# A four-layer graph network: strided sums in layer 0, own rows one tile ahead and an earlier check in layer 2

## The chip, the cores and the metric

The kernel runs on one core of one Trainium2 chip. The metric is device time in microseconds (us) of one execution. Five engines work side by side, each with its own queue of instructions kept in order: TensorE (PE, whose weight loads are shown apart as PEld), VectorE (DVE), ScalarE (ACT), GpSimd (POOL, which here issues the indirect DMAs) and SyncE (SP, which issues the plain ones). They wait for each other through semaphores.

## The reference

There are 3125 nodes with 128 features each and 100,000 edges, sorted by destination. Each edge has one of 500 relations, one of 8 types and three numbers. Four layers are applied in turn, each as `x = layernorm(x + layer(x))`:

```python
# layer 0: attention with 8 heads over a node's edges and the node itself
z_bar = segment_sum(z[edge_type], dst) / max(deg, 1)
pre_edge = (h @ P1)[dst] + (h @ P2)[src] + (z @ P3)[edge_type]
pre_self = h @ P1 + h @ P2 + z_bar @ P3
alpha = softmax of leaky(pre) @ y_w over the edges of dst and dst itself
t_edge = (h @ Wh)[src] + (z @ Wz)[edge_type];  t_self = h @ Wh + z_bar @ Wz
out = where(deg > 0, leaky(segment_sum(alpha * t) + residual_weight * h), h)
# layer 1: mean of x over the sources, then a two-layer perceptron
# layer 2: attention with 4 heads, one maximum for all edges
attn = leaky(sum(Q[dst] * K[src]) * SCALE + edge_attr @ We)
attn_exp = exp(attn - max(attn))
attn_norm = attn_exp / max(segment_sum(attn_exp, dst)[dst], 1e-12)
out = relu(concat([x, segment_sum(V[src] * attn_norm, dst) @ Wo + bo]) @ Wm + bm)
# layer 3: attention with one head; Q, K and V by node type, K also by edge type
```

Three sums over a node's edges in layer 0 matter here: that of the relations' rows z, for `z_bar`, made in two ways, and that of the weighted rows `alpha * t`.

## The kernel before, in words

The nodes are sorted by degree and padded to 3200, that is 25 tiles of 128 nodes, one node to a partition. A tile has as many slots for edges as its fullest node has edges: 57 for the first tile, 42, 40 and so on to 21 for the last, 821 in all. A chunk is eight slots (`W`); the last chunk of a tile may be smaller. Every layer goes through the 25 tiles in this order. `gather` (L89, whose instruction is L90) fetches one row per partition by an indirect DMA on POOL; `put` (L736, through `scatter`, L93) writes a tile's rows back by an indirect DMA. Edges beyond a tile's slots are worked through by `behind` (L641): a loop whose number of trips is loaded from memory (L647) and is zero for this input. The loop is still entered and left, and all engines meet at it.

A scheduler orders the instructions of every engine's queue from the program and its estimates of their times. Buffers come from pools; a tile of a pool with two buffers is written again only when its last but one user is done. In layer 0 the row buffers `hs` have eight, `zs` and most others two.

**Layer 0.** Beside its own work it counts edges between pairs of tiles for layer 1 (`counts`, L560 to L639, a generator that the main loop at L899 steps forward). Of each chunk the kernel gathers the rows of the sources into `hs`: 128 features for the logits, 128 for the message (the part `D:2 * D`) and 8 more. The relations' parts are made in two ways. In `gathered` (L801, 67 chunks, 45 of them full) rows `zs` are gathered from a table, added to `hs` (L808), and their last 64 columns are summed over the slots by `halved` (L809) and added to the tile's sum (L810). In `multiplied` (L819, 47 chunks, all full) one-hot matrices (L834, DVE) are multiplied by the relations (L838, PE) into `zT`, one block of 128 columns for each slot. PE then makes the logits' argument `pre` and the message's part `t_ps` (L849), which DVE adds to `hs` (L850). The eight blocks of `zT` are summed by L853, `halved` (L855) and, from a tile's second such chunk on, L857. Then come the logits (L787 to L790), the softmax (L669), and for each chunk `spread` (L868): the message part of `hs` is multiplied by the weights in place (L872), summed over the slots by `halved` (L873) and added to the tile's sum (L874). Then the tile's closing (L929 to L988) writes `x1` (the put at L977) and `u3`. The `prologue` of a tile (L768: a gather of x, its transpose at L711, two products) is called ahead of the last chunk of the tile before. `halved` is a tree of additions in place:

```python
while n > 2:
    k = n // 2
    V.tensor_add(v[:, :k], v[:, :k], v[:, n - k:n])
    n -= k
if n == 2:
    V.tensor_add(v[:, 0] if last is None else last, v[:, 0], v[:, 1])
```

For a full chunk that is four, two and one blocks: two instructions at L796 and one at L799. Elsewhere the kernel has a sum over the slots in one instruction, in `weigh` of layers 2 and 3 (`msg` at L696, the sum `u` at L700, its addition at L701).

**Layer 2.** It begins with a load of all edges' data (`pay_sb`, L1124) and 25 gathers of the tiles' own rows `xqb` (x and the query q; L1135). Then comes `behind` (L1166), then the loop over tiles (L1226): the query is prepared, rows `kv` are gathered by `rows2` (L1138), then logits, softmax and `weigh`. Last are `closing` (L1186), whose first transpose is that of `an` (L711, called at L1192), and `table3` (L1206), which makes the rows for layer 3 (L1222, L1223) and puts them (L1224). After the loop a check counts the nodes whose sum of weights, taken against the maximum over all nodes, falls under 1e-12 (L1249 to L1268). The count is loaded (L1269), and if it isn't zero, closings and tables are done again with the clamped sums (L1270); for this input it is zero. Layer 3 follows and reads the rows that were put.

Of the kernel before, what the change touches and what calls it, by code (L numbers as in the profile page):

```python
# [59 lines left out]
def segments(t):  # L60

    cs = chunks(t)
    n = -(-len(cs) // 5)
    runs = [cs[i * len(cs) // n:(i + 1) * len(cs) // n] for i in range(n)]
    return [(run[0][0], sum(run[-1]), run) for run in runs]
# [10 lines left out]
def tile_gnn(ctx, tc, a, out):  # L76
# [12 lines left out]
    def gather(dst, table, idx, **kw):  # L89
        return G.indirect_dma_start(out=dst, out_offset=None, in_=table, in_offset=indirect(idx), **kw)  # L90
# [612 lines left out]
    def query(ps, q):  # L703

        qp = ps.tile([P, D], F32, name="qp", bufs=2)
        A.activation(qp, q, AF.Copy)
        return qp
# [40 lines left out]
    with tc.tile_pool(name="l0", bufs=2) as wp, tc.tile_pool(name="l0s", bufs=1) as sp, \  # L748
# [40 lines left out]
            for s in range(k):  # L789
                T.matmul(lg_ps[:, s, :], low[:, s, :], yw8, start=True, stop=True)  # L790

        def halved(v, n, last=None):

            while n > 2:
                k = n // 2
                V.tensor_add(v[:, :k], v[:, :k], v[:, n - k:n])  # L796
                n -= k
            if n == 2:
                V.tensor_add(v[:, 0] if last is None else last, v[:, 0], v[:, 1])  # L799

        def gathered(h1T, idx, rl, n, za, lg_ps):  # L801

            hs = wp.tile([P, W, HC], F32, name="hs", bufs=8)
            zs = wp.tile([P, W, HC + R], F32, name="zs")
            for s in range(n):
                gather(hs[:, s, :], h_tab, idx(s))
                gather(zs[:, s, :], z_tab, rl[:, s:s + 1])
            V.tensor_add(hs[:, :n], hs[:, :n], zs[:, :n, :HC])  # L808
            halved(zs[:, :, HC:], n)  # L809
            V.tensor_add(za, za, zs[:, 0, HC:])  # L810
            for s0 in range(0, n, 4):
                k = min(4, n - s0)
                pre = ps.tile([P, 4, P], F32, name="pre")
                for s in range(k):
                    T.transpose(pre[:, s, :], hs[:, s0 + s, :D], ident)
                logits(pre, k, h1T, lg_ps[:, s0:s0 + k])
            return hs

        def multiplied(h1T, o, n, zbT, first, lg_ps):  # L819

            hs = wp.tile([P, W, HC], F32, name="hs", bufs=8)
            for s in range(n):
                gather(hs[:, s, :], h_tab, srcx[:, o + s:o + s + 1])
            rb = wp.tile([P, W * P], F16, name="rb")
            nc.sync.dma_start(rb[:, :n * P], rel_tab[o:o + n].rearrange("(o s) p -> o (s p)", o=1)
                              .to_broadcast([P, n * P]))
            zT = wp.tile([P, W * P], F32, name="zT")
            for s0 in range(0, n, 4):
                k = min(4, n - s0)
                cols = slice(s0 * P, (s0 + k) * P)  # L830
                oh = wp.tile([P, NK, 4 * P], BF16, name="oh")[:, :, :k * P]
                zps = ps1.tile([P, 4 * P], F32, name="zps")[:, :k * P]
                for i in range(NK):
                    V.tensor_scalar(oh[:, i], rb[:, cols], relid[:, i:i + 1], None, op0=OP.is_equal)  # L834
                    parts = [(zps, zq[:, i, :2 * R]), (zps[:R], zq[:, i, 2 * R:])]
                    for z, w in parts if i < NK - 1 else parts[::-1]:
                        whole = z is zps
                        T.matmul(z, w, oh[:, i], start=(whole and i == 0), stop=(whole and i == NK - 1))  # L838
                A.activation(zT[:, cols], zps, AF.Copy)
                pre = ps.tile([P, 4, P], F32, name="pre")  # L840
                T.matmul(pre[:, :k], zw[:, :D], zT[:, cols], start=True, stop=False)
                for s in range(k):
                    T.matmul(pre[:, s, :], hs[:, s0 + s, :D], ident, start=False, stop=(s == k - 1))  # L843
                logits(pre, k, h1T, lg_ps[:, s0:s0 + k])
            for s0 in range(0, n, 3):
                k = min(3, n - s0)
                t_ps = ps1.tile([P, 3, HC - D], F32, name="t_ps")
                for s in range(k):
                    T.matmul(t_ps[:, s, :], zT[:, (s0 + s) * P:(s0 + s + 1) * P], zw[:, D:], start=True, stop=True)  # L849
                V.tensor_add(hs[:, s0:s0 + k, D:], hs[:, s0:s0 + k, D:], t_ps[:, :k])  # L850
            assert n == W
            zh = wp.tile([P, W // 2, P], F32, name="zh")
            V.tensor_add(zh, zT.rearrange("z (s p) -> z s p", p=P)[:, :W // 2],  # L853
                         zT.rearrange("z (s p) -> z s p", p=P)[:, W // 2:])
            halved(zh, W // 2, zbT if first else None)  # L855
            if not first:
                V.tensor_add(zbT, zbT, zh[:, 0])  # L857
            return hs

        def masked(lg_ps, hss, n, mk):  # L860
# [7 lines left out]
        def spread(ac, hs, ex, n):  # L868

            val = hs[:, :n, D:2 * D]  # L870
            valh = val.rearrange("p s (h d) -> p s h d", h=H)
            V.tensor_tensor(valh, valh, ex.unsqueeze(3).to_broadcast([P, n, H, D // H]), op=OP.mult)  # L872
            halved(hs[:, :, D:2 * D], n)  # L873
            V.tensor_add(ac, ac, hs[:, 0, D:2 * D])  # L874

        def behind0(t, pl, mk, rl):
            _, _, h1T = prologue(t)
# [247 lines left out]
    with tc.tile_pool(name="l2", bufs=2) as wp, tc.tile_pool(name="l2s", bufs=1) as sp, \  # L1125
# [6 lines left out]
        l = sp.tile([P, NT, H2], F32, name="l")  # L1132
        V.memset(l, 0.0)
        V.memset(accb, 0.0)
        for t in range(NT):  # L1135
            gather(xqb[:, t, :], xq_tab, od.ids(t))

        def rows2(qp, pl, n, lg):  # L1138
            kv = wp.tile([P, W, 2 * D], F32, name="kv", bufs=8)
            for s in range(n):  # L1140
# [15 lines left out]

        def behind2(t, pl, mk, rl):
            lg = wp.tile([P, max(CAP), H2], F32, name="lg")
            kv = rows2(query(ps1, qb[:, t, :]), pl, W, lg[:, :W])
            biased(pl, W, lg[:, :W], mk)  # L1160
            ex = ps1.tile([P, max(CAP), H2], F32, name="ex")
            corr = softmax(wp, lg[:, :W], W, H2, m[:, t, :], l[:, t, :], ex[:, :W])
            faded(accb[:, t, :], corr, H2)
            weigh(wp, accb[:, t, :], kv[:, :, D:], ex[:, :W], W, H2)
# [41 lines left out]
        def table3(t):  # L1206
# [16 lines left out]
            A.activation(rows[:, :, D:], qkv[:, 2 * D:].unsqueeze(1).to_broadcast([P, NET, D]), AF.Copy)  # L1223
            put(ktv_tab, od, t, rows.rearrange("p e f -> p (e f)"))  # L1224

        for t in range(NT):  # L1226
            qp = query(ps1, qb[:, t, :])
            for s0, s1, run in segments(t):
                lg = wp.tile([P, max(CAP), H2], F32, name="lg")
                parts = []  # L1230
                for c0, w in run:
                    o = OFF[t] + c0
                    parts.append(rows2(qp, pay_sb[:, o:o + w], w, lg[:, c0 - s0:c0 - s0 + w]))
                n, o = s1 - s0, OFF[t] + s0
                biased(pay_sb[:, o:o + n], n, lg[:, :n], mask[:, o:o + n])
                ex = ps1.tile([P, max(CAP), H2], F32, name="ex")
                corr = softmax(wp, lg[:, :n], n, H2, m[:, t, :], l[:, t, :], ex[:, :n])
                faded(accb[:, t, :], corr, H2)
                for (c0, w), kv in zip(run, parts):
                    weigh(wp, accb[:, t, :], kv[:, :w, D:], ex[:, c0 - s0:c0 - s0 + w], w, H2)  # L1240

            rl = wp.tile([P, H2], F32, name="rl")
            V.tensor_scalar(rl, l[:, t, :], 1e-12, None, op0=OP.max)
            V.reciprocal(rl, rl)
            closing(t, rl)
            table3(t)


        mx = sp.tile([P, 1], F32, name="mx_all")  # L1249
        V.tensor_reduce(mx, m, AX.XY, OP.max)  # L1250
        mt = ps1.tile([P, P], F32, name="tp")
        T.transpose(mt, mx.to_broadcast([P, P]), ident)
        top = sp.tile([P, 1], F32, name="top")
        V.tensor_reduce(top, mt, AX.X, OP.max)
        f = sp.tile([P, NT, H2], F32, name="f")
        V.tensor_scalar(f, m, top, None, op0=OP.subtract)
        A.activation(f, f, AF.Exp)
        has2 = sp.tile([P, NT, H2], F32, name="has2")
        V.tensor_scalar(has2, l, 0.0, None, op0=OP.is_gt)
        V.tensor_mul(l, l, f)  # L1260
        few = sp.tile([P, NT, H2], F32, name="few")
        V.scalar_tensor_tensor(few, l, 1e-12, has2, op0=OP.is_lt, op1=OP.mult)
        few1 = sp.tile([P, 1], F32, name="few1")
        V.tensor_reduce(few1, few, AX.XY, OP.add)
        few_ps = ps1.tile([1, 1], F32, name="few_ps", tag="tp")
        T.matmul(few_ps, few1, ones[:, :1], start=True, stop=True)
        fewi = sp.tile([1, 1], I32, name="fewi")
        V.tensor_copy(fewi, few_ps)  # L1268
        again = nc.values_load(fewi, min_val=0, max_val=NP * H2)  # L1269
        with tc.If(again > 0):  # L1270
            V.tensor_scalar(l, l, 1e-12, None, op0=OP.max)
# [78 lines left out]
```

## Time and profile before

| what | us |
|---|---|
| median of 3 runs (lowest, highest) | 5862.23 (5854.55, 5864.28) |
| the profiled execution | 5814.11 |
| its span, first to last instruction | 5812.4 |
| sorting, tables, up to layer 0 | about 0 to 206 |
| layer 0 with its counts | about 206 to 3045 |
| layer 1 | about 3045 to 3223 |
| layer 2 | about 3223 to 4586 |
| layer 3 | about 4586 to 5812 |

The page gives an engine's busy time and share of the span. A group of instructions is a line of the kernel, an engine, an operation and the tiles it writes and reads; it shows its count, its total and mean duration, and what ended the idle time of the engine before it ("issue" is time in which nothing that the profile shows was waited for). Start times are us from the span's first instruction. The mean granted clock of TensorE is 0.588 of full speed. The times by stage are read from the timeline of the one profiled execution, which is 48 us below the median of the runs.

### The profile page before, as it was taken

The page shows a single profiled execution, that of the slowest core. Times are in us where ns is not written, and L with a number is a line of the kernel's source. Part 1 is how long each engine was busy: PE and PEld are TensorE (multiplying, and loading weights), DVE is VectorE, ACT ScalarE, POOL GpSimd, SP SyncE. Part 2 cuts the span into 40 slices and gives each one's busy share as a digit, 9 for nine tenths or more (in the row PEclk, how much of TensorE's full clock was granted, in tenths as well). Part 3 has the DMA queues.
Part 4 walks back from the last instruction along what each step waited for, and adds up shares of the span by engine and source line. Part 5 has one row for each costly group of instructions (what it writes and reads, how often), then busy time and mean ns, then how long its engine had stood idle before and what let it go on. Part 6 is the DMA issues. An engine that isn't in the chain of part 4 may idle for free. (4 is left out here: it accounts for less than half of the span.)

```text
span 5812.4 us, 36204 instructions
## 1 busy us (share of the span) xinstructions
PE 2236.2 (38%) x10027; PEld 1363.8 (23%) x10027; DVE 3104.1 (53%) x6976; ACT 934.1 (16%) x2437; POOL 3074.3 (53%) x3136
## 2 busy tenths in 40 slices
PE   7165545555556556576658112222233200000000
PEld 5143333333334334344433001111111100000000
DVE  8354555554455446565652346565656455545555
ACT  1031222221222222222211001111111100000000
POOL 0555545545453544444640566566656366666664
PEclk9565556555665666566569555555555555555555
DMA  2423322322222222222335333333333233333332
GB/s 80 120 75 85 88 75 76 86 74 80 74 81 70 80 76 79 82 76 79 102 92 196 106 95 107 99 110 114 104 100 107 72 96 92 90 93 93 94 89 66
DMA packets 220239, 530.60 MB, mean 91 GB/s; under 512 B 65690, under 2 KB 112461, under 8 KB 215386
## 3 DMA queue, kind: packets, MB, share of 16 engines
q0 software_dynamic: 147968, 437.97, 26.6%
q1 hardware_dynamic: 72024, 89.90, 4.7%
q8 instruction: 87, 1.43, 0.1%
q14 instruction: 160, 1.30, 0.1%
HBM read 457.09 MB, written 70.63 MB: 91 GB/s over the span
## 5 line engine op out<-in xcount | busy, mean ns | idle before, releaser
L90 POOL DMA_INDIRECT hs<-h_tab,srcx x821 | 880.0, 1072 | 602.1 <-issue 448.7
L90 POOL DMA_INDIRECT kv<-kv_tab,pay_sb x821 | 782.1, 953 | 421.7 <-issue 239.5
L90 POOL DMA_INDIRECT kv<-ktv_tab,pay_sb x821 | 778.8, 949 | 332.3 <-issue 258.1
L90 POOL DMA_INDIRECT zs<-z_tab,rel x445 | 466.8, 1049 | 695.4 <-DVE az L810 303.3
L628 PE MATMUL c_ps<-c_ohs,c_ohd 128*128 128x128 bf16 x1300 | 334.3, 410 | 299.1 <-issue 110.3
L700 DVE TENSOR_REDUCE u<-msg 128x128 f32<-128x1024 f32 (+4 forms) x228 | 384.2, 1685 | 114.3 <-remote 69.6
L838 PE MATMUL zps<-oh,zq 128*128 128x512 bf16 x752 | 339.7, 516 | 88.3 <-DVE oh L834 80.1
L790 PE MATMUL lg<-yw,low 128*128 128x8 f32 x1642 | 306.4, 316 | 125.8 <-ACT low L788 81.6
L790 PEld LDWEIGHTS lg<-yw,low 128*128 128x128 f32 x1642 | 305.2, 276 | 162.8 <-ACT low L788 104.0
L628 PEld LDWEIGHTS <-c_ohd 128*128 128x128 bf16 x1300 | 187.2, 147 | 431.7 <-issue 256.2
L1295 DVE TENSOR_TENSOR qk<-kv,qp 128x1024 f32<-128x1024 f32 (+4 forms) x114 | 126.4, 1109 | 289.1 <-DMA kv<-ktv_tab,pay_sb 242.8
L623 DVE TENSOR_TENSOR c_ohs<-c_ends,c_up 128x1024 bf16<-128x1024 bf16 (+4 forms) x193 | 118.9, 616 | 248.0 <-remote 111.8
L696 DVE TENSOR_TENSOR msg<-kv,ex 128x1024 f32<-128x1024 f32 (+4 forms) x228 | 249.1, 1104 | 0.0
L604 ACT ACTIVATE c_oha<-c_oha,srclo 128x50 bf16<-128x50 bf16 (+2 forms) x821 | 201.5, 327 | 258.8 <-DVE c_oha L600 189.5
L850 DVE TENSOR_TENSOR hs<-hs,t_ps 128x408 f32<-128x408 f32 x141 | 74.5, 528 | 300.2 <-remote 193.0
L787 DVE TENSOR_TENSOR low<-pre,h1T 128x512 f32<-128x512 f32 (+1 forms) x215 | 141.3, 660 | 166.9 <-PE pre L843 76.1
L630 ACT ACTIVATE c_sb<-c_ps 128x512 bf16<-128x512 f32 (+1 forms) x175 | 96.5, 552 | 802.2 <-remote 363.0
L1143 DVE TENSOR_TENSOR qk<-kv,qp 128x1024 f32<-128x1024 f32 (+4 forms) x114 | 126.1, 1107 | 181.6 <-DMA kv<-kv_tab,pay_sb 173.1
L849 PE MATMUL t_ps<-zw,zT 128*128 128x136 f32 x752 | 153.7, 338 | 151.1 <-issue 105.1
L711 PE MATMUL tp<-ident,xk 128*128 128x128 f32 x100 | 42.3, 423 | 426.7 <-DVE xk L1211 88.6
L711 PE MATMUL tp<-ident,an 128*128 128x128 f32 x25 | 11.5, 461 | 434.5 <-DVE msg L696 174.3
L788 ACT ACTIVATE low<-low 128x512 f32<-128x512 f32 (+1 forms) x215 | 128.9, 606 | 274.7 <-DVE low L787 246.1
(394 smaller groups left out, 5252.7 us busy)
## 6 DMA issues: line engine op xcount, KB each, us to landing
c_tab<-c_sb SPq DMA_DIRECT2D x25, 768.0 KB
cs<-c_tab SPq DMA_DIRECT2D x6, 3200.0 KB
hs<-h_tab,srcx POOLq DMA_INDIRECT x821
kv<-kv_tab,pay_sb POOLq DMA_INDIRECT x821
kv<-ktv_tab,pay_sb POOLq DMA_INDIRECT x821
rb<-rel_tab SPq DMA_DIRECT2D x47, 256.0 KB
zs<-z_tab,rel POOLq DMA_INDIRECT x445
h_tab<-h SPq DMA_DIRECT2D x25, 132.0 KB
```

The lines of the kernel that those rows point to most:

```text
L90: return G.indirect_dma_start(out=dst, out_offset=None, in_=table, in_offset=indirect(idx), **kw)
L604: A.activation(oha[:, s, 0, :], oha[:, s, 1, :], AF.Copy, scale=srclo[:, o:o + 1])
L628: T.matmul(cps[:, j * P:(j + 1) * P], ohd[:, :, nb * j + i], ohs[:, :, nb * j + i], start=(i == 0), stop=(i == nb - 1))
L696: V.tensor_tensor(msg[:, :n, :].rearrange("p s (h d) -> p s h d", h=heads), val.rearrange("p s (h d) -> p s h d", h=heads), ex.unsqueeze(3 ...
L700: V.tensor_reduce(u, msg[:, :n, :].rearrange("p s d -> p d s"), AX.X, OP.add)
L787: V.tensor_add(low[:, :k], pre[:, :k], h1T.unsqueeze(1).to_broadcast([P, k, P]))
L788: A.activation(low[:, :k], low[:, :k], AF.Relu)
L790: T.matmul(lg_ps[:, s, :], low[:, s, :], yw8, start=True, stop=True)
L838: T.matmul(z, w, oh[:, i], start=(whole and i == 0), stop=(whole and i == NK - 1))
L849: T.matmul(t_ps[:, s, :], zT[:, (s0 + s) * P:(s0 + s + 1) * P], zw[:, D:], start=True, stop=True)
L1143: V.tensor_mul(qk[:, :n], kv[:, :n, :D], qp.unsqueeze(1).to_broadcast([P, n, D]))
L1295: V.tensor_mul(qk[:, :n], kv[:, :n, :D], qp.unsqueeze(1).to_broadcast([P, n, D]))
```

## The change

It has three parts. In layer 0, `halved` is replaced by `summed`, a single reduction over the slots with the slots as innermost axis, read with a stride, into a small tile of its own (`zr`, `zh`, `hr`; the first `zT` chunk of a tile goes straight to `zbT`). The addition to the tile's sum stays; for `zT` the first halving, which was written apart as L853, is within the reduction now. In layer 2, the 25 gathers of own rows no longer stand in front of `behind`: tile 0's stands ahead of the loop over tiles, and that of tile t + 1 follows the query of tile t; the body of `behind` gathers its own. And the check becomes a function that is called in the last tile of the loop, in front of that tile's `closing`.

```diff
@@ layer 0
-        def halved(v, n, last=None):
-
-            while n > 2:
-                k = n // 2
-                V.tensor_add(v[:, :k], v[:, :k], v[:, n - k:n])
-                n -= k
-            if n == 2:
-                V.tensor_add(v[:, 0] if last is None else last, v[:, 0], v[:, 1])
+        def summed(to, rows):
+
+            V.tensor_reduce(to, rows.rearrange("p s d -> p d s"), AX.X, OP.add)
...
-            halved(zs[:, :, HC:], n)
-            V.tensor_add(za, za, zs[:, 0, HC:])
+            zr = wp.tile([P, R], F32, name="zr")
+            summed(zr, zs[:, :n, HC:])
+            V.tensor_add(za, za, zr)
...
-            zh = wp.tile([P, W // 2, P], F32, name="zh")
-            V.tensor_add(zh, zT.rearrange("z (s p) -> z s p", p=P)[:, :W // 2],
-                         zT.rearrange("z (s p) -> z s p", p=P)[:, W // 2:])
-            halved(zh, W // 2, zbT if first else None)
+            zh = zbT if first else wp.tile([P, P], F32, name="zh")
+            summed(zh, zT.rearrange("z (s p) -> z s p", p=P))
             if not first:
-                V.tensor_add(zbT, zbT, zh[:, 0])
+                V.tensor_add(zbT, zbT, zh)
...
-            halved(hs[:, :, D:2 * D], n)
-            V.tensor_add(ac, ac, hs[:, 0, D:2 * D])
+            hr = wp.tile([P, D], F32, name="hr")
+            summed(hr, val)
+            V.tensor_add(ac, ac, hr)
@@ layer 2
-        for t in range(NT):
-            gather(xqb[:, t, :], xq_tab, od.ids(t))
...
         def behind2(t, pl, mk, rl):
             lg = wp.tile([P, max(CAP), H2], F32, name="lg")
+            gather(xqb[:, t, :], xq_tab, od.ids(t))
...
+        def check():
+
+            mx = sp.tile([P, 1], F32, name="mx_all")
...
+            V.tensor_copy(fewi, few_ps)
+            return f, fewi
+
+        gather(xqb[:, 0, :], xq_tab, od.ids(0))
         for t in range(NT):
             qp = query(ps1, qb[:, t, :])
+            if t + 1 < NT:
+                gather(xqb[:, t + 1, :], xq_tab, od.ids(t + 1))
             for s0, s1, run in segments(t):
...
+            if t == NT - 1:
+                f, fewi = check()
             closing(t, rl)
             table3(t)
...
-        mx = sp.tile([P, 1], F32, name="mx_all")
...
-        V.tensor_copy(fewi, few_ps)
         again = nc.values_load(fewi, min_val=0, max_val=NP * H2)
```

The lines left out in `check()` are those of the check before, unchanged.

More of the change, by code (lines that the diff above doesn't have):

```diff
@@ L1224, in table3 @@
             put(ktv_tab, od, t, rows.rearrange("p e f -> p (e f)"))
+        def check():
+            mx = sp.tile([P, 1], F32, name="mx_all")
+            V.tensor_reduce(mx, m, AX.XY, OP.max)
+            mt = ps1.tile([P, P], F32, name="tp")
+            T.transpose(mt, mx.to_broadcast([P, P]), ident)
+            top = sp.tile([P, 1], F32, name="top")
+            V.tensor_reduce(top, mt, AX.X, OP.max)
+            f = sp.tile([P, NT, H2], F32, name="f")
+            V.tensor_scalar(f, m, top, None, op0=OP.subtract)
+            A.activation(f, f, AF.Exp)
+            has2 = sp.tile([P, NT, H2], F32, name="has2")
+            V.tensor_scalar(has2, l, 0.0, None, op0=OP.is_gt)
+            V.tensor_mul(l, l, f)
+            few = sp.tile([P, NT, H2], F32, name="few")
+            V.scalar_tensor_tensor(few, l, 1e-12, has2, op0=OP.is_lt, op1=OP.mult)
+            few1 = sp.tile([P, 1], F32, name="few1")
+            V.tensor_reduce(few1, few, AX.XY, OP.add)
+            few_ps = ps1.tile([1, 1], F32, name="few_ps", tag="tp")
+            T.matmul(few_ps, few1, ones[:, :1], start=True, stop=True)
+            fewi = sp.tile([1, 1], I32, name="fewi")
+            V.tensor_copy(fewi, few_ps)
+            return f, fewi
+        gather(xqb[:, 0, :], xq_tab, od.ids(0))
         for t in range(NT):
             qp = query(ps1, qb[:, t, :])
+            if t + 1 < NT:
+                gather(xqb[:, t + 1, :], xq_tab, od.ids(t + 1))
             for s0, s1, run in segments(t):
@@ L1244, in tile_gnn @@
             V.reciprocal(rl, rl)
+            if t == NT - 1:
+                f, fewi = check()
             closing(t, rl)
             table3(t)
-        mx = sp.tile([P, 1], F32, name="mx_all")
[L1250 to L1267, printed above, removed]
-        V.tensor_copy(fewi, few_ps)
         again = nc.values_load(fewi, min_val=0, max_val=NP * H2)
```

## The prediction

> **What bounds the kernel now.** I read the page first, then stages, waits, order of time. The page's totals fit no engine as the bound:
>
> ```profile
> PE 2236.2 (38%) x10027; PEld 1363.8 (23%) x10027; DVE 3104.1 (53%) x6976; ACT 934.1 (16%) x2437; POOL 3074.3 (53%) x3136
> ```
>
> The sums belong to layer 0 (206 to about 3045 us). The chain of waits is followed back only to 3220 us, so layer 0 is read from windows: busy us of PE, PEld, DVE, ACT, POOL in each 500 us.
>
> ```profile
> 500.00:1000.00 500.00, 287.99 (x1408) 189.08 (x1408) 279.39 (x657) 126.01 (x335) 243.58 (x229) 0.60 0.29 80
> 2500.00:3000.00 500.00, 322.73 (x1468) 210.25 (x1466) 292.14 (x806) 123.90 (x313) 268.84 (x258) 0.62 0.34 91
> ```
>
> No engine reaches two thirds: the period of a tile is set by queues kept in order that wait for each other in turn. The waits of layer 0 (total, times, longest):
>
> ```profile
> POOL hs L90 <- issue: 448.7, 778, 46.5
> POOL zs L90 <- DVE az L810: 303.3, 17, 30.8
> ...
> PE tp L711 <- DMA x<-in_x,node_d: 102.2, 7, 25.4
> ...
> PE zps L838 <- DVE oh L834: 80.1, 16, 13.2
> ```
>
> POOL stands until DVE has freed a row buffer; PE then stands for the x rows that POOL gathers behind those rows, and for a one-hot (L834) that stands on DVE behind a tile's sums. DVE's timeline shows such a burst (start, duration):
>
> ```profile
> 1523.21 2.35 DVE L872 TENSOR_TENSOR hs<-hs,lgs 128x1024 f32<-128x1024 f32 x2
> 1525.48 1.95 DVE L796 TENSOR_TENSOR hs<-hs 128x512 f32<-128x512 f32 x4
> 1527.35 0.48 DVE L799 TENSOR_TENSOR hs<-hs 128x128 f32<-128x128 f32 x2
> 1527.76 0.28 DVE L874 TENSOR_TENSOR az<-az,hs 128x128 f32<-128x128 f32 x1
> ...
> 1534.18 0.35 DVE L834 TENSOR_SCALAR oh<-rb,relid 128x512 bf16<-128x512 f16 x1
> ```
>
> By start times, four L796 take 1.87 us and two L799 0.41: 1.14 us per chunk of eight slots. The first L874 ends at 1528.04; POOL's next row gather starts at 1528.78. The L834 ends at 1534.53, PE's zps starts at 1534.58 after 12.3 us of waiting. So DVE's burst is on the path in some tiles, and POOL's rows and x in the others.
>
> **What the Trainium skill says.** "VectorE: DVE Perf Modes", section "The perf-mode tier table (the rule you actually need)", gives tensor_reduce its 1x mode alone, as it does fp32 tensor_tensor. The trace agrees: over 1024 contiguous elements, a reduce takes 1211 ns (L1296), a multiply 1217 (L872). "SBUF — State Buffer", section "Specifications (TRN2)", has 16-byte lines with a penalty for each crossing to a new one. A reduce over slots crosses at every element, and here it is dearer:
>
> ```profile
> L700 DVE TENSOR_REDUCE u<-msg 128x128 f32<-128x1024 f32 x184 | 344.0, 1869 | 101.6 <-remote 64.7 <-issue 23.3 <-DVE msg L696 7.3
> L1296 DVE TENSOR_REDUCE lg<-qk 128x8 f32<-128x1024 f32 x92 | 111.4, 1211 | 32.5 <-remote 13.6 <-issue 10.2 <-DVE lg L681 3.4
> L796 DVE TENSOR_TENSOR hs<-hs 128x512 f32<-128x512 f32 x92 | 61.5, 682 | 0.0
> ```
>
> "Perfetto Trace Analysis", section "Optimizing Scalar/DVE Operations", has some 60 ns of overhead per DVE instruction, with about half the profiled latency overlapped by the next. That speaks for fewer instructions, and the trace agrees: L874 lasts 281 ns, the next starts after 0.20 us.
>
> **Part 1, layer 0's sums.** Removed: the halvings (L796, L799) and the zh add (L853). Added: one strided reduce each. The nearest row is L700, the same operation, axis and size: 1869 ns for 1024 elements, 1012 for 512. Successors start about 0.08 us before a predecessor's end, so they occupy 1.78 and 0.93 us of the queue.
> - hs, 92 full chunks: 1.78 - 1.14 = 0.64 each, 59 us. 22 partial ones, priced as four slots: 0.93 - (0.33 + 0.20) = 0.40 each, 9 us.
> - zT, 47 chunks: 1.78 - (0.61 + 0.33 + 0.20) = 0.64 each, 30 us.
> - zs, 45 full chunks of 512 elements: 0.93 - (0.33 + 0.20 + 0.13) = 0.27 each, 12 us; 22 partial ones at half that, 3 us.
>
> Together 113 us more of DVE, although some 408 instructions go (two fewer in most chunks). Bounds: at L1296's rate the sums would cost 1.13 us against 1.14 and the part nothing; the row means without overlap (+0.48 us x 92 and so on) give 79. I take 113, since L700's form is the same.
>
> How much is on the path? Following layer 0's timeline backwards tile by tile I put about a half of it on PE and 28% on DVE, with some 60 to 77% of the halvings in those DVE stretches; but a delay there is partly taken up by a wait with another releaser. I choose a half: +56 us. Against it, the new order of DVE interleaves two multiplies and the sum: the first buffer comes free after 2 x 1.13 + 1.78 = 4.04 us of a burst instead of 2 x 1.13 + 1.87 + 0.41 + 0.20 = 4.74, 0.7 us earlier. Over 24 tiles that is 17 us where POOL's wait decides, and I take half: -8. The changed program also has other orders: POOL puts a tile's remaining rows ahead of the next x gather, by 2 to 8 gathers in about half of the first twelve tiles (1.25 us each), but its last zs gathers before the x1 put; PE's transpose of x stands later in tiles 7 to 15. Each can help or hurt: 0, with +/-35 us for the range. Layer 0: **+48**.
>
> **Part 2, layer 2's own rows.** Before, all 25 gathers stand on POOL ahead of the loop's entry, which waits until the last has landed; then come the first edge rows:
>
> ```profile
> 3249.68 8.48 DMA xqb<-xq_tab,node_d
> ...
> 3262.02 0.66 issue
> 3262.68 0.94 POOL kv L90
> ```
>
> Gathers start 1.25 us apart, 3223.33 to 3253.44. In the changed order POOL meets the loop first, then 12 own-row gathers, 57 rows, 1, 32, 12, and so on. DVE's `left` (L646), which the loop's trip loading follows, ends at 3226.0. In layer 3 the same ends at 4589.15 and rows start at 4592.45: 3.3 us. So gathers could start at 3229.3 and edge rows 12 x 1.25 later, at 3244.3: 18 us earlier. If the entry also waits for the 2463 KB load of pay_sb (issued 3222.52, landed by 3230 to 3233), it is 11 to 14. I take **-14**. The other 13 gathers, 16.3 us of POOL, stand by row 90 and later; POOL waits 19.12 us at tile 0's put (3455.58) for rows whose chain left POOL at row 81 (3362.82), so they are hidden. Were that cover gone, they would cost up to 16 and the part be about nil.
>
> **Part 3, the check.** Before, it runs beside the last rows (L1222, 4576.5), the put and its landing, 4577.92 to 4583.01; its result (4579.31) is awaited by nobody, since POOL goes on only after the landing: moving it saves 0. After, its PE transpose and matmul stand ahead of the last closing's transpose of `an`, and its DVE block ahead of that closing's L1202; ACT loads tables for its exp.
>
> ```profile
> 4559.84 0.12 PE tp L711
> ...
> 4577.92 5.09 DMA ktv_tab<-rows,node_d
> ```
>
> Its DVE chain lasts about 2.2 us (4577.09 to 4579.31) and can start once the previous tile's rows (L1222) end at 4560.56; then `an`'s transpose stands at about 4562.7 instead of 4559.8: **+3**, between 0 (it runs in DVE's idle time) and +5 (two table loads of 1.28 us shown). Behind it are ACT's copies, PE's projections and the put.
>
> **Sum:** 48 - 14 + 3 = +37. The profiled execution is 5814.11 us (span 5812.4), so 5851 on its scale; it is 48 us below the median of the runs, 5862.23, to which I add the difference: **5899**.
>
> **Rivals.**
> 1. Hidden sums, which ends on the other side. If the loop of POOL's rows, x and PE sets each tile, DVE's extra work fills its 45% idle time and the earlier release counts in full: -17 - 14 + 3 = -28, 5834. For: 448.7 us of POOL's waits and PE's 102.2 for x. Against: PE's waits for L834, at the end of bursts that grow by 0.64 us x 4 chunks. It decides where under (17 + 14 - 3)/113, a quarter, of the added time is on the path.
> 2. Full cost: the chain through DVE closes in every tile, +113 - 14 + 3 = +102, 5964. For: POOL's 303.3 us for DVE's L810, which the dearer zs sum precedes. Against: the x waits.
> 3. They cancel: a sixth on the path (+19) and -8, -14, +3 give 0, 5862. The change then does what it says and nothing is seen of it.
>
> **Numbers.** A measurement of this kernel can tell about 0.2% (12 us) from no change. Forecast 0.45 (own range 5872 to 5935), hidden 0.27, full 0.14, cancelled 0.14. Faster: 0.23 of the hidden case and 0.02 of the cancelled, 0.25. Same: 0.01, 0.04 and 0.07, 0.12. The rest, 0.63, slower. The range from 5836 to 5955 leaves out about 0.12 of the hidden case and 0.08 of the full one.
>
> **What would show it.** Right: strided sums of 1.85 us in layer 0 for hs and zT, DVE's busy time there up by about 80 us, layer 0's end about 48 us later; the first edge row of layer 2 about 14 us sooner after the first own row's former start, and POOL's 19 us wait at the first put kept or grown; the last put 3 us later after the previous tile's rows. Wrong: sums near 1.2 us; a tile period unchanged while DVE's busy share grows; own rows that wait for something else and delay the edge rows; or a layer 0 that moves by more than 35 us through POOL's and PE's new order alone.

## The result, and the profile after

The changed kernel takes 5906.24 us (median of 6 runs, 5892.24 to 5933.12), the kernel before 5855.52 us beside it (6 runs): ratio 1.0092, 95% interval 1.0073 to 1.0111, slower by some 54 us on the ratio (the medians alone are 51 us apart). The profiled execution of the changed kernel takes 5892.24 us, its span is 5890.4. That is 78 us more than the profiled execution before, whose time lay below all six runs of its kernel above; shares of the difference are taken from ratios, traces serve to find the places.

The page's first lines after (busy us, share, instructions):

```profile
PE 2226.4 (38%) x9959; PEld 1369.5 (23%) x10027; DVE 3229.0 (55%) x6568; ACT 936.2 (16%) x2438; POOL 3009.5 (51%) x3136
```

DVE has 408 instructions less and is busy 125 us longer. The groups of the new sums, by shape (count, total us, mean ns):

```profile
L794 DVE TENSOR_REDUCE hr<-hs 128x128 f32<-128x1024 f32 x92 | 181.6, 1986 | 0.0
...
L794 DVE TENSOR_REDUCE zr<-zs 128x64 f32<-128x512 f32 x45 | 48.1, 1070 | 0.0
L794 DVE TENSOR_REDUCE zbT<-zT 128x128 f32<-128x1024 f32 x25 | 47.4, 1895 | 51.6 <-issue 47.0 <-ACT zT L835 4.6
L794 DVE TENSOR_REDUCE zh<-zT 128x128 f32<-128x1024 f32 x22 | 42.4, 1927 | 0.0
```

These are as dear as L700, that of hs somewhat dearer. A burst at the end of a tile on DVE's timeline:

```profile
1534.28 2.35 DVE L866 TENSOR_TENSOR hs<-hs,lgs 128x1024 f32<-128x1024 f32 x2
1536.55 3.85 DVE L794 TENSOR_REDUCE hr<-hs 128x128 f32<-128x1024 f32 x2
1540.32 0.28 DVE L869 TENSOR_TENSOR az<-az,hr 128x128 f32<-128x128 f32 x1
...
1547.64 0.58 DVE L794 TENSOR_REDUCE hr<-hs 128x128 f32<-128x384 f32 x1
...
1548.54 0.34 DVE L830 TENSOR_SCALAR oh<-rb,relid 128x512 bf16<-128x512 f16 x1
```

The first one-hot (L830, before L834) comes 14.3 us after the burst's start, before it came 11.0 us after. The first buffer is free when the first L794 ends, about 1538.5, 4.3 us after the burst's start (before 4.8); POOL's next row gather starts at 1539.26. Two stretches of layer 0, columns as before:

```profile
500.00:1000.00 500.00, 272.44 (x1366) 183.17 (x1374) 289.27 (x556) 118.40 (x311) 229.79 (x225) 0.60 0.28 78
...
2500.00:3000.00 500.00, 286.69 (x1325) 187.44 (x1337) 277.69 (x644) 116.63 (x302) 220.04 (x227) 0.62 0.30 82
```

The last stretch shows the loss: PE does 287 us of work in it instead of 323. The waits of layer 0 (206 to 3110 us):

```profile
POOL hs L90 <- issue: 537.0, 792, 40.2
...
POOL zs L90 <- DVE zr L794: 396.5, 34, 37.2
...
PE zps L834 <- DVE oh L830: 81.9, 15, 18.2
...
PE tp L711 <- DMA x<-in_x,node_d: 19.8, 1, 19.8
```

Such a list splits a wait by the instruction that ended it, and a changed program gives it other names. The groups on the two pages have the whole idle time in front of POOL's gathers (after the second bar), first before, then after:

```profile
L90 POOL DMA_INDIRECT hs<-h_tab,srcx x821 | 880.0, 1072 | 602.1 <-issue 448.7
L90 POOL DMA_INDIRECT zs<-z_tab,rel x445 | 466.8, 1049 | 695.4 <-DVE az L810 303.3
```

```profile
L90 POOL DMA_INDIRECT hs<-h_tab,srcx x821 | 833.6, 1015 | 673.5 <-issue 537.0
L90 POOL DMA_INDIRECT zs<-z_tab,rel x445 | 445.6, 1001 | 650.9 <-DVE zr L794 396.5
```

In front of the row gathers `hs` POOL stands 71 us longer. In front of `zs` it stands 45 us less in all, though the part put down to DVE's sum of `zs` has grown (303 to 397). PE's wait for the x rows has nearly gone as a name (102 to 20 us); all idle time in front of that transpose fell by less, from 160 to 119 us. PE's wait for the one-hot has not grown (80 and 82 us). Stages, from the starts of the puts in the two traces (us):

| | before | after | difference |
|---|---|---|---|
| last x1 put of tile 16 (layer 0) | 2468.7 | 2467.6 | -1 |
| last x1 put of layer 0 | 3040.9 | 3108.3 | +67 |
| first edge row of layer 2 | 3262.7 | 3317.1 | +54 |
| first put of layer 2 | 3455.6 | 3511.0 | +55 |
| second put of layer 2 | 3525.7 | 3602.8 | +77 |
| third put of layer 2 | 3566.8 | 3636.1 | +69 |
| last put of layer 2 | 4577.9 | 4652.7 | +75 |
| last put of layer 3 | 5803.1 | 5881.2 | +78 |

Layer 0 lost all its time behind tile 16, although most of DVE's added work lies before it. In these last tiles DVE's waits whose releaser the trace can't name (remote) grew from 45 to 130 us. Layer 2 won 13 us at its first edge row, was 10 us behind at its second put, and 2 us behind at its third.

### The profile page after: what moved, and what is told of

It is laid out like the page before. It is cut to its first block, busy times and chain, and to the rows that moved or that the text cites. A ratio compares the mean times of both kernels' runs of the same rounds, so it can differ in the third digit from the quotient of the medians.

```text
span 5890.4 us, 35699 instructions
## 1 busy us (share of the span) xinstructions
PE 2226.4 (38%) x9959; PEld 1369.5 (23%) x10027; DVE 3229.0 (55%) x6568; ACT 936.2 (16%) x2438; POOL 3009.5 (51%) x3136
## 5 line engine op out<-in xcount | busy, mean ns | idle before, releaser
L90 POOL DMA_INDIRECT hs<-h_tab,srcx x821 | 833.6, 1015 | 673.5 <-issue 537.0
L90 POOL DMA_INDIRECT zs<-z_tab,rel x445 | 445.6, 1001 | 650.9 <-DVE zr L794 396.5
L700 DVE TENSOR_REDUCE u<-msg 128x128 f32<-128x1024 f32 (+4 forms) x228 | 384.2, 1685 | 131.4 <-remote 76.4
L834 PE MATMUL zps<-oh,zq 128*128 128x512 bf16 (+1 forms) x696 | 316.8, 520 | 87.7 <-DVE oh L830 81.9
L794 DVE TENSOR_REDUCE hr<-hs 128x128 f32<-128x1024 f32 (+4 forms) x114 | 202.4, 1786 | 0.0
```

Of the source, the lines that this page charges most:

```text
L700: V.tensor_reduce(u, msg[:, :n, :].rearrange("p s d -> p d s"), AX.X, OP.add)
L794: V.tensor_reduce(to, rows.rearrange("p s d -> p d s"), AX.X, OP.add)
```

## The experiments

They ran on chips that differ. On most of them the kernel before takes 5815 to 5872 us (the first kind), on one 5145 to 5166 us (the second kind). Every ratio is taken against the kernel before, run beside it on the same chip.

### The parts one by one

Layer 0's sums alone: the diff's first four hunks on the kernel before.

> Layer 0's strided sums alone, layer 2 as before. If the sums carry the whole difference and layer 2's two parts cancel, 5855 + 54 = 5909 (ratio 1.009). If layer 2 gains what the forecast said (-14 + 3), the sums alone must cost more: 5920 (1.011). Under 1.006 would mean that layer 2 itself makes the changed kernel slower.

Measured: 5859.95 us against 5815.48, ratio 1.0076 (1.0056 to 1.0097). The sums make nearly all of it, as the first case has it; 1.011 is excluded.

The own rows alone:

```diff
-        for t in range(NT):
-            gather(xqb[:, t, :], xq_tab, od.ids(t))
...
+        gather(xqb[:, 0, :], xq_tab, od.ids(0))
         for t in range(NT):
             qp = query(ps1, qb[:, t, :])
+            if t + 1 < NT:
+                gather(xqb[:, t + 1, :], xq_tab, od.ids(t + 1))
...
```

> Layer 2's own-row gathers alone. Forecast's reason (13 later gathers hidden behind POOL's wait at the first put): -14, ratio 0.9976, first edge row 13 to 14 us sooner and every put of layer 2 as much sooner. Rival, gain given back: the first edge row is sooner, but from tile 1 on the puts stand where they stood, ratio 1.000; in the changed kernel's trace the puts' lead of 12 us at tile 0 was gone at tile 1. Second rival: that loss belonged to that one execution, in which DVE and ACT had gaps of about 1 us between instructions for 45 us, and is not seen here.

Measured: ratio 0.9999 (0.9988 to 1.0011), 5814.50 us; a gain of 14 us (0.9976) is excluded. The gaps named as the second rival came again at the same instructions with the same lengths, so they do not belong to one execution. Against the last x1 put, the first edge row starts 208.3 us later instead of 221.8, and the first put 402.4 instead of 414.7; the second put stands 494.8 us later instead of 484.8, the third 528.0 instead of 525.9.

The check alone, with its lines moved into `check()` unchanged:

```diff
...
+            if t == NT - 1:
+                f, fewi = check()
             closing(t, rl)
             table3(t)
```

> The check's move alone. Forecast's reason: +3 us on the path from the last closing to the last put, ratio 1.0005, only to be seen in the trace: the last closing's transpose of an stands behind the check's matmul. Rival: it runs in idle time of DVE and PE, 0.

Measured: ratio 1.0012 (1.0002 to 1.0022), 5821.17 us: slower, by 1 to 13 us. The interval holds the 3 us of the forecast. PE's timeline around the last closing shows them, before:

```profile
4556.29 3.55 PE L1221 MATMUL e_ps<-wed,kT 128*128 128x512 f32 x4 [0.78 <-ACT kT L713]
4559.67 0.27 PE L711 MATMUL tp<-ident,an 128*128 128x128 f32 x1
```

and in the changed kernel:

```profile
4628.72 1.98 PE L1214 MATMUL e_ps<-wed,kT 128*128 128x512 f32 x4 [0.92 <-ACT kT L713]
4630.54 0.27 PE L1224 MATMUL tp<-ident,mx_all 128*128 128x128 f32 x1
4633.19 0.19 PE L1238 MATMUL few_ps<-ones,few 128*1 128x1 f32 x2 [2.38 <-DVE few L1236]
4633.62 0.33 PE L711 MATMUL tp<-ident,an 128*128 128x128 f32 x1 [0.24 <-DVE fewi L1240]
```

Before, the transpose of `an` follows the e_ps matmuls directly. If it did so here, it would stand where that of `mx_all` stands, at 4630.54; it waits for DVE's check and starts at 4633.62.

### Duration or order

The sums' duration can be changed with the order kept, if each full sum reads eight neighbouring columns (near reads): the traces show the same sequence of instructions as in the changed kernel on DVE (6568), ACT (2438) and POOL (3136). On PE some records are missing from one of the traces; in the repeat below the sequence is the same there too.

```diff
-            V.tensor_reduce(to, rows.rearrange("p s d -> p d s"), AX.X, OP.add)
+            n = rows.shape[1]
+            if n == 8:
+                V.tensor_reduce(to.rearrange("p (s g) -> p s g", s=8), rows.rearrange("p s (g e) -> p s g e", e=8), AX.X, OP.add)
+            else:
+                V.tensor_reduce(to, rows.rearrange("p s d -> p d s"), AX.X, OP.add)
```

> The changed kernel, whose sums over eight slots read eight neighbouring columns instead of one column of eight slots (a different sum: layer 0's relation sums and messages are then not the reference's; the addresses read and their number are the same). The order of instructions is that of the changed kernel on every engine; only the durations of these sums fall, from 1.99, 1.9 and 1.07 us to some 1.2, 1.2 and 0.65. Theory 1, duration: half of 113 us was on the path, so it returns to about 5855 - 11 = 5845, ratio 0.997 to 1.000. Theory 2, order: the new order of PE, ACT and POOL in layer 0 makes the loss (the trace of the changed kernel lost its time in tiles 17 to 23 alone), so it stays at 5900, ratio 1.008 to 1.010. Between: a share for each.

Measured: ratio 1.0042 (1.0028 to 1.0056), 5838.97 us. The full sums of hs fell to 1208 ns (group by shape), and DVE's busy time stands in the page's first line:

```profile
L796 DVE TENSOR_REDUCE hr<-hs 128x128 f32<-128x1024 f32 x92 | 110.0, 1208 | 0.0
```

```profile
PE 2240.8 (38%) x10027; PEld 1364.4 (23%) x10027; DVE 3110.9 (53%) x6568; ACT 934.4 (16%) x2438; POOL 3013.0 (52%) x3136
```

All sums together take 221.5 us instead of 343.8. About half of the loss went with the 122 us; the other half stayed, although DVE is busy no longer than with the halvings (3110.9 and 3104.1 us). Neither theory alone.

The opposite: the order of the kernel before, with dearer halvings (the same sequence on DVE, ACT and POOL as before).

```diff
-                V.tensor_add(v[:, :k], v[:, :k], v[:, n - k:n])
+                lo, hi = v[:, :k], v[:, n - k:n]
+                if k >= 2:
+                    lo, hi = (q.rearrange("p s d -> p d s") for q in (lo, hi))
+                V.tensor_add(lo, lo, hi)
...
-            V.tensor_add(zh, zT.rearrange("z (s p) -> z s p", p=P)[:, :W // 2],
-                         zT.rearrange("z (s p) -> z s p", p=P)[:, W // 2:])
+            V.tensor_add(zh.rearrange("z s p -> z p s"), zT.rearrange("z (s p) -> z p s", p=P)[:, :, :W // 2],
+                         zT.rearrange("z (s p) -> z p s", p=P)[:, :, W // 2:])
```

> The kernel before and its order of instructions, with the halvings of four and two blocks (and zh's first) going through their elements slots innermost, so that each takes longer by its strides; results as before. From the reduction, strides cost (1986 - 1208)/1024 = 0.76 ns for each element read; a chunk's 768 additions would cost 0.6 to 1.2 us more, all chunks together 90 to 190 us of DVE. If a quarter of DVE's added time is on the path, as in the changed kernel with and without near reads (0.5% or 29 of 122 us), ratio 1.004 to 1.008. If a half is, as forecast, 1.008 to 1.016. If DVE's time is hidden in this order of instructions and only the changed order makes it count, 1.000.

Measured, on the chip of the second kind: ratio 1.0038 (1.0025 to 1.0052), 5165.96 us. A full addition of hs takes

```profile
L799 DVE TENSOR_TENSOR hs<-hs 128x512 f32<-128x512 f32 x92 | 94.0, 1038 | 0.0
```

instead of 682 ns, and the groups together 99 us more. The kernel lost 20 us, all of it in layer 0 (its last put there stands 21.7 us later than in the next kernel, which has the old halvings and ran on the same chip): a fifth, by the interval 13 to 27%.

On the same chip, own rows kept out of tile 0's and tile 1's edge rows (shown against the own-rows kernel above; called the gated kernel below):

```diff
-            if t + 1 < NT:
-                gather(xqb[:, t + 1, :], xq_tab, od.ids(t + 1))
+            if t == 0:
+                gather(xqb[:, 1, :], xq_tab, od.ids(1))
+            elif t + 1 < NT:
+                one = wp.tile([P, 1], F32, name="one")
+                V.tensor_scalar(one, l[:, t - 1, 0:1], -1.0, None, op0=OP.is_gt)
+                idn = wp.tile([P, 1], I32, name="idn")
+                V.scalar_tensor_tensor(idn, od.ids(t + 1), 0.0, one, op0=OP.add, op1=OP.mult)
+                gather(xqb[:, t + 1, :], xq_tab, idn)
```

> The kernel before, with own rows gathered one tile ahead in fact: from tile 2 on each gather takes its row numbers from a small tile that DVE writes after the sums of weights of the tile before last, so that POOL meets one own-row gather behind each put of rows, not twelve in front of the edge rows and thirteen among those of tile 1. First edge row some 26 us sooner than in the kernel before. Theory, the thirteen gathers took POOL's slack: the lead at tile 0's put is kept at tile 1, ratio 0.996 to 0.998. Rival, layer 2 is bound by a chain through DVE from tile 1 on and takes back any lead of POOL: 1.000, and the lead is again gone at tile 1 or 2. Third: one gather behind each put stands ahead of the edge rows for which DVE waits, 24 x 1.25 = 30 us, ratio up to 1.003.

Measured: 1.0039 (1.0025 to 1.0052), 5162.37 us: slower. Against the last x1 put its first edge row stands 28 us earlier than in the kernel with strided halvings (194.6 and 223.1 us), its first put 27 us earlier (370.2 and 397.1), its last put 11 us later (1404.8 and 1393.4). The theory held for the first puts: without the twelve gathers in front of tile 1's later rows, the second put still stands 31 us earlier (432.7 and 463.9). Further on the lead is lost. The third case, one gather behind each put, fits in size (24 x 1.25 = 30 of some 40 us), but is not shown: the edge rows on POOL are divided among the puts in another way too, and DVE has 46 instructions more than before.

And the changed kernel with near reads for hs alone (`summed` reads as above where its last argument is true):

```diff
...
-            summed(hr, val)
+            summed(hr, val, True)
```

> The changed kernel and its order of instructions, with the sums of the weighted rows (hr, 92 full chunks) alone reading eight neighbouring columns (a different sum: layer 0's messages are then not the reference's); those of zT and zs stay strided. All sums together fell by 122 us of DVE and gave back 0.5% of 0.9%; hs's fall is 92 x 0.78 = 72 us of the 122. If what counts is DVE's time as such, 1.009 - 0.005 x 72/122 = 1.006. If the burst at a tile's end is what PE and POOL wait for, nearly all of it comes from hs: 1.004. If it is the sums of zs and zT, in the middle of a tile: 1.008 to 1.009.

Measured: 5078.00 us against 5144.86, ratio 0.9872 (0.9857 to 0.9887), outside all three cases: faster than the kernel before. Layer 0's last put stands at 2544.5 us, 72 us before that of the gated kernel, whose layer 0 is the old one; yet DVE is busy 49 us longer (3127.5 and 3078.6). So on this chip the new order wins, where it loses on the others.

### On other chips

The next four ask whether the sign of the whole change turns with the chip. Their chip was of the first kind, so this stayed open: the changed kernel itself has no run on the second kind.

> The changed kernel again. The runs so far fell on two kinds of chip: on the first two the kernel before takes 5815 to 5856 us and the trace has some 1500 us of waits whose releaser it can't name (remote); on the third it takes 5145 us and has 20 us of them. On a chip of the first kind: 1.009 again. On one of the second kind: near reads of hs alone gave 0.987 there; with a quarter of the 72 us of its strides on the path 0.991, with all of it 1.001. So the sign of the change would depend on the chip.

Measured: 5935.66 us against 5871.85, ratio 1.0118 (1.0095 to 1.0142).

> Layer 0's strided sums alone again. On a chip of the first kind 1.0076 as before. On one of the second kind: layer 2's parts are worth about nothing there too (the lead of 15 us at the first edge row was gone at the first put in the trace of the near reads), so the same as the changed kernel within 0.2%: 0.990 to 1.001. If layer 2's parts make the difference there, 1.000 or more here and less in the changed kernel.

Measured: 1.0099 (1.0075 to 1.0123), 5923.89 us.

> Layer 2's own-row gathers alone again. First kind of chip: 1.000 again. Second kind: forecast's reason (13 later gathers hidden) 0.9974; rival (POOL is the bound of layer 2's beginning, 13 x 1.25 = 16 us come back): 1.000.

Measured: 0.9995 (0.9978 to 1.0011), 5867.99 us.

> The changed kernel with all its full sums reading eight neighbouring columns, as before. First kind of chip: 1.0042 again, 0.5% under the changed kernel. Second kind: if strides count as they do there (a quarter on the path), 0.6% under the changed kernel, about 0.985; if they are hidden without the stalls, the same as the changed kernel and as the near reads of hs alone (0.987).

Measured: 1.0054 (1.0032 to 1.0077), 5896.09 us. Here the changed kernel and its near reads ran on one chip: 1.0118 - 1.0054 = 0.64%, 38 us of the 122, which is 31%. The two intervals together leave some 15 to 45%.

The last ran on the chip of the second kind again, not on the first as its text hopes:

> The near reads of hs's sums alone again, hoped for on a chip of the first kind (kernel before above 5800 us). There the changed kernel has 1.009 to 1.012 and all near reads 1.004 to 1.005, 0.5 to 0.6% between them. If DVE's time as such counts, hs gives back its part of the strides, 72 of 122 us: 1.006 to 1.008. If only the burst at a tile's end counts, nearly all: 1.004 to 1.006. If only the sums of zs and zT count: 1.009 to 1.012. On a chip of the second kind 0.987 again.

Measured: 5089.25 us against 5165.70, ratio 0.9855 (0.9834 to 0.9876). It repeats the gain; how much of the strides' cost is hs's stays open. PE's wait for x in layer 0 is 261 us in this kernel and 308 us with the strided halvings on the same chip, whose order is the old one. On chips of the first kind it is 102 us before and 20 after.

## Why the prediction was right or wrong

It gave 5899 from 5862 us, +37; measured are +54 (43 to 65). The direction was right, and dearer sums are about half of the reason, as the near reads show. Most of the rest is the new order, which the sum put at nothing. That the total came near is in part luck: with what was measured the terms are some +38 for the strides, +20 for the order, 0 for the own rows and +3 to +7 for the check, 61 to 65 where 54, and 69 on the second chip, were measured. In the forecast, too large a share of DVE's time was partly made up by taking the order, the release and the own rows too well.

- **The sums' durations**: right. 1863 ns were forecast, 1986 (hs) and about 1910 (zT) found; 113 us more DVE were worked out from spacings, 125 us show on the page. The 80 us named among the signs of being right is the other way of counting, by the sums' own durations; so counted it came to 92 (343.8 and 252 us), and an overlap of about 0.08 us with the next instruction, for each of the 408 that went, fits the other 33. (0.08 of L874's 0.28 us is not the half that the prediction takes as borne out.)
- **A half of it on the path**: too much. "I choose a half: +56 us" was read from how much of layer 0's backward timeline lay on DVE. Taking the strides away in the changed order gives back 31% of them (the changed kernel and its near reads on the chip of 5872 us; on the chip of 5815 us, from the sums alone and with the check taken off, 0.45% or 21%). Adding strides to the old order costs a fifth of them, on the second kind of chip. At 31%, 113 us are 35 us. The remark that "a delay there is partly taken up by a wait with another releaser" may be the reason; no run separates it.
- **The new order: 0, with +/-35 us**: the sum's biggest miss in the other direction. With DVE no busier than before, the order kept 0.42 to 0.54%, of which the check has 0.12; some 20 us remain. It is not one effect: up to tile 16 the new order was not slower, in the tiles after it it was. It was so with near reads too: on the chip of 5872 us the near-reads kernel is 11 us ahead of the own-rows kernel, whose layer 0 is the old one, at tile 16's x1 put and 29 us behind it at the last, 40 us lost in between.

  In these last tiles DVE's waits without a named releaser are 42 to 76 us in the four traces of the first kind with the old order and 99 to 130 us in the six with the new one; on the second kind there are none, and the new order wins there as well. That ties the loss to these waits but doesn't prove it, for in the tiles before they grew too, without a loss. What they are, and which instruction's place brings them, was not taken apart.

  On the second kind of chip the whole layer became 72 us shorter: there the sign of being wrong, "a layer 0 that moves by more than 35 us" through the order alone, did come.
- **The earlier release, -8**: the first buffer is free 0.6 us earlier in the burst shown (0.7 forecast), but POOL stood longer in front of the row gathers (602 to 674 us). No gain was seen; it can't be told apart from the order.
- **Own rows, -14**: the first step was right, the first edge row came 13 us earlier. "So they are hidden" failed: 0.9999 and 0.9995. Before and after, POOL at the first put and the next row:

```profile
3455.58 0.99 POOL L93 DMA_INDIRECT ktv_tab<-rows,node_d  x1 [19.12 <-issue]
3459.96 0.96 POOL L90 DMA_INDIRECT kv<-kv_tab,pay_sb  x1 [3.39 <-DVE msg L696]
```

```profile
3510.99 0.99 POOL L93 DMA_INDIRECT ktv_tab<-rows,node_d  x1 [4.05 <-issue]
3523.79 0.96 POOL L90 DMA_INDIRECT kv<-kv_tab,pay_sb  x1 [11.80 <-remote]
```

  The wait in front of the put took twelve gathers in (19.12 to 4.05 us), and the put kept 12 us of the lead. (So the sign "kept or grown" for this wait was wrong by the forecast's own reason.) But those twelve stand ahead of row 89 (rows counted from 0), and rows 89 to 138 follow each other on POOL 0.30 us apart, with no wait to give up. Against the last x1 put, rows up to 88 stand 11.7 us earlier than before and row 89 stands 3.3 us later. It is the same on the second kind of chip, where POOL has no wait at the first put: the lead of the near reads of hs (last run) over the strided halvings is 15.9 us at the first edge row, 14.3 at row 80 and -1.1 at row 89. What the forecast took for hidden was hidden from one put, not from the rows behind.

  On the first kind the second put is thrown back further. DVE, on which the next row's buffer waits, shows gaps in front of instructions that wait only for DVE itself:

```profile
3519.36 0.16 DVE L686 TENSOR_TENSOR l<-l,sm 128x4 f32<-128x4 f32 x1 [4.83 <-remote]
...
3523.55 1.87 DVE L700 TENSOR_REDUCE u<-msg 128x128 f32<-128x1024 f32 x1 [1.77 <-remote]
```

  All traces of the first kind with this change have the same five gaps of over 1 us within 26 us of the first put, some 17.6 us together; those without it have one, of 3.9 us. The trace names no releaser, and what they are stays open. They do not decide what the part is worth: on the second kind there are none, and the third put ends at nearly the same, 1.4 us behind there and 0.6 to 2 us on the first kind.
- **The check, +3**: right, 3.1 us in the trace; alone it cost 1 to 13 us.
- **Rivals**: hidden sums (5834) did not come, nor did the third rival, that the effects cancel: the interval excludes no change. The limit of hidden sums, a quarter of the added time on the path, is not excluded, with 21 and 31% measured; what it counted on beside that, a release of 17 and a lead of 14 us, did not come, and the order cost some 20. On the second kind a kernel with most of the change is faster. Full cost (5964) is excluded: the interval ends at some 5920.

## What to carry to other kernels

A sum over slots by one strided reduction costs 1.9 to 2.0 us where three halvings cost 1.14, so fewer instructions are no gain by themselves. Where a scheduler orders the queues, replacing instructions moves others too: separate both by a kernel that changes durations alone, with the order kept, before an explanation is believed. Work moved behind the start of a stage is hidden only if what stands behind it on its engine can wait; here the rows behind the twelve gathers paid the lead of 13 us back. And compare the whole idle time in front of a group, not the part with one releaser's name: a changed program renames it.

## What the runs showed of the hardware

- The same kernel took 5815 to 5872 us on most chips and 5145 to 5166 on another. The strided sum of zT into zbT lasts 1895 ns on both; the waits differ. The kernel before has at least 1490 us of waits for a releaser that the trace can't name (remote) on the first kind, the strided-halvings kernel, with the same order, 20 us on the second. The longest group of each in layer 0:

```profile
ACT c_sb L630 <- remote: 363.0, 25, 54.9
```

```profile
ACT zT L842 <- remote: 20.2, 6, 5.3
```

  The new order of layer 0 is a loss on the first kind and a gain on the second.
- Strides cost a two-operand addition too: 512 elements in 1038 instead of 682 ns, when slots are innermost.
- A reduction of 1024 elements that reads 1056 bytes apart (hs) takes 1986 ns, 512 bytes apart 1869 (L700) to 1927 (zT), neighbours 1208.
